# Reordering the first loads of a four-layer gated cross-attention kernel: eight small bias loads issued by ScalarE, the second and third context blocks ahead of most weights

## Chip, cores and metric

The kernel runs as one program on one core of a Trainium2 chip. The metric is the device time of one launch in microseconds (us), as the median of several runs. The core has five engines that run their own instruction streams: PE (TensorE: matmuls, with weight loads shown as PEld), DVE (VectorE), ACT (ScalarE), POOL (GpSimd) and SP (SyncE, which here only issues DMAs; its instruction queue is written SPq).

## What is computed

Four layers, each a gated cross-attention followed by a gated feed-forward block, on `x` of 16 batches of 128 tokens by 256 features, all in float32. Only the first attention matters for this change:

```
xn = layernorm(x)                                # per token, over 256 features
Q = xn @ Wq + bq;  K = ctx @ Wk + bk;  V = ctx @ Wv + bv       # 16 heads of 16
A = softmax(Q K^T / 4)
x = x + tanh(g_xattn[0]) * ((A V) @ Wo + bo)
```

After it follow a routed expert block (top 1 of 8), a second attention with a mask and an added bias, a routed block with top 2 of 8 and a shared expert, a third attention, a soft mixture over 64 experts, a fourth attention with heads of 64, and a product-key block.

## The kernel before

All 16 batches of `x` stay in SBUF as tiles `x0` to `x15` of 128 x 256. The context comes transposed, in four blocks of 512 columns (`ctxT`, block g holds batches 4g to 4g+3). The attention weights of a layer stand in one DRAM array `aw`, and are loaded into one large tile `aw` piece by piece.

**The loads.** `load_attention(0, load_others)` (L131) issues the first layer's loads, all on SP's queue, in the order in which they are written: the key weights (L135, 512 KB), context block 0 (L126, 512 KB), `x0` and `x1` (L58, 128 KB each), the two rows of gates (L63, L64), eight loads of query and key biases (L148, 16 partitions with 4 separate elements of 4 bytes each), the query weights (L151, 512 KB), the value weights (L152, 256 KB), the value bias and the output bias, each broadcast to all partitions (L153, L155), and then `load_others` (L178): `x2`, `x3`, context block 1, `x4`, `x5`, block 2, `x6`, `x7`, block 3, `x8`, `x9`. Eight loads of the output weights (L159) and `x10` to `x15` come last.

A load that the queue issues marks its end on one of eight completion slots, which are handed out in turn. A load whose slot was used before waits, in its issuing queue, until the load that had the slot has landed. All that stand behind it in the queue wait too.

**The work at the start.** POOL packs the key weights and later the query weights (L165). For each context block, `keys` (L436) multiplies packed key weights by the block into two PSUM banks `pk` (L442, four matmul instructions, each seen as two in the trace because the data are float32), and ACT adds the key bias into `kraw` (L445). POOL splits the keys into two masked halves `kT` (L454). For each batch: DVE takes mean and variance (L199, L201), POOL makes the reciprocal root (L194, L195), DVE writes the normalised tile `xn` (L226), POOL adds the gated output bias into `x` (L521), PE transposes `xn` (L237, `pt`), and ACT copies that out (L241). Then come queries (L461, L471), value rows (L487, L494), scores (L532), row maxima (L544), exponentials on ACT (L566), normalisation on POOL (L579), transposes (L585), values (L601), output (L617) and the gated sum (L259).

**The order.** In `xattn16` (L411) the order on each engine is written out by hand: a list of stages, each with a lag in batches, run under a manual schedule. Keys are in it ahead of everything: the order on PE is keys of block 0, keys of block 1, transpose of batch 0, keys of block 2, transpose of batch 1, keys of block 3, queries of batches 0 and 1, transpose of batch 2, value rows of batch 0, scores of batch 0. DVE scales the query bias (L171) and multiplies the output bias by the gate (L172) ahead of the first `xn`. POOL packs the query weights ahead of the first `kT` and the first reciprocal root. Engines run their instructions strictly in this order.

Of the kernel before, what the change touches and what calls it, by code (L numbers as in the profile page):

```python
# [22 lines left out]
NG, GT = 4, 512  # L23
# [13 lines left out]
def flamingo_gated(ctx: ExitStack, tc: tile.TileContext, a, out):  # L37
    nc = tc.nc
# [12 lines left out]
    def broadcast(ap, n):  # L51
        return ap.rearrange("(o n) -> o n", o=1).to_broadcast([P, n])
# [4 lines left out]
    def load_x(b):  # L57
        nc.sync.dma_start(out=xb[b], in_=a["x"][b])  # L58
# [3 lines left out]
    def load_gates():  # L62
        nc.sync.dma_start(out=gates[:, 0:4], in_=broadcast(a["g_xattn"], 4))  # L63
        nc.sync.dma_start(out=gates[:, 4:8], in_=broadcast(a["g_ffn"], 4))  # L64
        nc.scalar.activation(gates, gates, AF.Tanh)

    def gate_x(layer):
        return gates[:, layer : layer + 1]
# [55 lines left out]
    def load_context(g):  # L124
        t = ctxp.tile([P, 2, GT], F32, tag="ctxT", name="ctxT")
        nc.sync.dma_start(out=t, in_=a["ctxT"][:, :, g * GT : (g + 1) * GT])  # L126
        ctxT[g] = t
# [3 lines left out]
    def load_attention(layer, between=None):  # L131

        t = wp.tile([P, WSLOT], F32, tag="w", name=f"aw{layer}")
        src = a[f"aw{layer}"]
        nc.sync.dma_start(out=t[:, 1024:2048], in_=src[:, 1024:2048])  # L135
        if between is not None:
            load_context(0)
            for b in range(2):
                load_x(b)
            load_gates()  # L140
        bqk = t[:, 3328:3332].rearrange("p (n c) -> p n c", n=2)
        wo = t[:, 2560:3072].rearrange("p (c m) -> p c m", c=2)
        blocks = []
        for i in range(2):
            for j in range(4):
                blocks.append((i, slice(64 * i + 16 * j, 64 * i + 16 * (j + 1)), src[32 * j : 32 * j + 16, :]))
        for i, r, part in blocks:
            nc.sync.dma_start(  # L148
                out=bqk[r], in_=part[:, 3584:3592].rearrange("p (n c i) -> p n c i", n=2, c=2)[:, :, :, i]
            )  # L150
        nc.sync.dma_start(out=t[:, 0:1024], in_=src[:, 0:1024])  # L151
        nc.sync.dma_start(out=t[:, 2048:2560], in_=src[:, 2048:2560])  # L152
        nc.sync.dma_start(out=t[:, 3340:3596], in_=broadcast(a[f"bv{layer}"], D))  # L153
        tgbo = t[:, 3072:3328]
        nc.sync.dma_start(out=tgbo, in_=broadcast(a[f"bo{layer}"], D))  # L155
        if between is not None:
            between()
        for i, r, part in blocks:
            nc.sync.dma_start(  # L159
                out=wo[r], in_=part[:, 2560:3584].rearrange("p (c i m) -> p c i m", c=2, i=2)[:, :, i, :]  # L160
            )
        packed = {}
        for n, at in ((1, 3600), (0, 1024)):
            w = t[:, at : at + 512]
            nc.gpsimd.tensor_copy(  # L165
                w.rearrange("p (g d) -> p g d", d=16),
                t[:, n * 1024 : (n + 1) * 1024].rearrange("p (g s) -> p g s", s=32)[:, :, 0:16],
            )
            packed[n] = w.rearrange("p (c m) -> p c m", c=2)
        bq = t[:, 3332:3334]  # L170
        nc.vector.tensor_scalar(bq, bqk[:, 0, :], 0.25, None, ALU.mult)  # L171
        nc.vector.tensor_scalar(tgbo, tgbo, gate_x(layer), None, ALU.mult)  # L172
        aw[layer] = dict(
            wq=packed[0], wk=packed[1], wv=t[:, 2048:2560].rearrange("p (c m) -> p c m", c=2), wo=wo,
            bq=bq, bk=bqk[:, 1, :], bv=t[:, 3340:3596], tgbo=tgbo,
        )

    def load_others():  # L178
        for b in range(2, 10):
            load_x(b)  # L180
            if b % 2:
                if b // 2 < NG:
                    load_context(b // 2)

    load_attention(0, load_others)
    for b in range(10, B):
        load_x(b)
# [1408 lines left out]
    def attention1(after, joining):  # L1596
        load_attention(1)
        with tc.tile_pool(name="rel", bufs=3) as rp:
            loaded = {}

            def load(b):
                m = rp.tile([P, S], a["mask"].dtype, tag="m", name="m")
                nc.sync.dma_start(out=m, in_=a["mask"][b])
                r = rp.tile([P, S], F32, tag="r", name="r")
                nc.sync.dma_start(out=r, in_=a["rel"][b])
                loaded[b] = m, r

            def mask(b):
                mf = rp.tile([P, S], F32, tag="mf", name="mf")
                nc.gpsimd.tensor_scalar(mf, loaded[b][0], -1.0, HUGE, ALU.add, ALU.mult)  # L1610
                return mf

            def make(b, mf):
                r = loaded.pop(b)[1]
                f = rp.tile([P, 1], F32, tag="f", name="f")
                nc.vector.tensor_reduce(f, mf, AX.X, ALU.max)
                nc.vector.tensor_scalar(f, f, -1.0, None, ALU.is_ge)
                nc.vector.scalar_tensor_tensor(r, r, 0.25, mf, ALU.mult, ALU.add)
                return r, f

            xattn16(1, (load, mask, make), after, joining)
# [18 lines left out]
    def attention2(after, joining):  # L1640
        load_attention(2)
        xattn16(2, after=after, joining=joining)
# [99 lines left out]
```

## Time and profile before

| | us |
|---|---|
| median of three runs | 2056.13 (2055.76 to 2060.23) |
| the profiled execution | 2059.8 |
| its span, first to last instruction | 2058.1 |
| PE busy in the span | 1854.9 (90%) |
| DVE, ACT, POOL busy | 1257.9, 912.3, 791.2 |

The profile is of one execution. Times in it count from the start of the span. A timeline line reads: start, length, engine, line of the program, operation, result and operands, shapes, number of instructions merged; in square brackets the idle time of the engine ahead of it, and what ended that. A line of the waits view reads: engine and line that waited, what ended the wait, then us in total, times, and the longest. In a table by stretches, "PEclk" is the granted share of full TensorE clock and the last two columns are the mean busy share of the 16 DMA engines and the GB/s that they moved.

### The profile page before, as it was taken

What the parts mean: (1) busy time and instruction counts of PE and PEld (TensorE: products, weight loads), DVE (VectorE), ACT (ScalarE), POOL (GpSimd) and SP (SyncE); (2) the same over time, 40 slices, a digit from 0 to 9 for tenths busy, and PEclk for the clock granted to TensorE, in tenths of its full rate; (3) what the DMA queues carried; (4) which work ended last, traced back from release to release, by engine and by line L of the source; (5) the groups of instructions that cost most, each with busy time, mean ns of one, the idle gap of its engine ahead of it and who ended that gap; (6) DMA issues with size and microseconds to landing.
All of it is one profiled execution on the core that took longest, in us unless ns stands there. A gap on an engine that the chain in (4) does not pass through costs nothing.

```text
span 2058.1 us, 31016 instructions
## 1 busy us (share of the span) xinstructions
PE 1854.9 (90%) x10345; PEld 1242.7 (60%) x10345; DVE 1257.9 (61%) x3763; ACT 912.3 (44%) x3002; POOL 791.2 (38%) x952
## 2 busy tenths in 40 slices
PE   6996899979879999989979989868999999998787
PEld 3774566557636566657744434357776677775775
DVE  3885122478752222249859999699717666663797
ACT  4993222489911222249931122244324434333673
POOL 4873332377510455448832222200102222220785
PEclk9997999998889999999999999989999999999799
DMA  3003777310010688861031123433200000000000
GB/s 118 14 17 111 283 292 283 113 31 27 17 75 1 252 321 315 308 230 37 2 115 79 75 109 143 181 144 120 82 1 1 1 1 1 22 1 1 6 17 21
DMA packets 52720, 204.19 MB, mean 99 GB/s; under 512 B 11600, under 2 KB 31568, under 8 KB 41552
## 3 DMA queue, kind: packets, MB, share of 16 engines
q0 software_dynamic: 13872, 121.12, 16.1%
q1 hardware_dynamic: 38688, 81.07, 11.2%
q8 instruction: 84, 1.38, 0.3%
q14 instruction: 76, 0.62, 0.1%
HBM read 171.75 MB, written 30.41 MB: 98 GB/s over the span
## 4 chain that ended last, share of the span: by engine, by line
PE 27%; DVE 20%; issue 3%; ACT 3%; POOL 2%; DMA 1%; SPq 0%; POOLq 0%; ACTq 0%; DVEq 0%
PE pk L287 3%; PE pq L299 3%; PE po L382 3%; PE pv L310 3%; DVE tot L1317 2%; DVE rep L1523 2%; PE acc L1280 2%; PE po L1337 2%; PE av L372 2%; DVE cw L1311 1%; PE sc L329 1%; PE pq L1419 1%; DVE cw L1319 1%; PE pe L358 1%; PE pl L1254 1%
## 5 line engine op out<-in xcount | busy, mean ns | idle before, releaser
L922 PE MATMUL pg<-we,xT 128*128 128x512 f32 (+1 forms) x528 | 243.1, 590 | 2.4 <-ACT xT L211 2.4
L579 POOL TENSOR_TENSOR e<-e,sums 128x512 f32<-128x512 f32 x192 | 199.6, 1071 | 67.4 <-DVE sums L574 28.4
L928 DVE TENSOR_TENSOR h<-sg,pg 128x256 f32<-128x256 f32 x132 | 54.3, 411 | 237.7 <-ACT sg L927 190.1
L566 ACT ACTIVATE e<-sc,mx 128x128 f32<-128x128 f32 x512 | 181.5, 421 | 17.3 <-DVE mx L544 16.3
L927 ACT ACTIVATE sg<-pg 128x256 f32<-128x256 f32 x132 | 49.7, 376 | 270.3 <-PE pg L922 260.3
L888 POOL DMA_INDIRECT we<-in_we,rows x56 | 54.0, 964 | 265.6 <-PE pd L953 165.2
L350 POOL TENSOR_TENSOR e<-e,rec 128x512 f32<-128x512 f32 x64 | 65.3, 1041 | 219.0 <-DVE rec L349 155.2
L922 PEld LDWEIGHTS pg<-we,xT 128*128 128x128 f32 x528 | 96.2, 194 | 82.2 <-issue 72.1
L1337 PE MATMUL po<-yt,cT 128*128 128x256 f32 x512 | 126.1, 391 | 11.2 <-ACT cT L1329 11.1
L1280 PE MATMUL acc<-d,k 128*128 128x512 f32 x256 | 123.1, 623 | 13.9 <-POOL d L1270 13.5
L566 ACT ACTIVATION_READ_ACCUMULATOR e<-sc,mx 128x1 f32 x512 | 132.9, 260 | 0.0
L585 PE MATMUL pe<-ident,e 128*128 128x128 f32 x768 | 103.7, 279 | 32.0 <-DVE mx L549 17.4
L1270 POOL TENSOR_TENSOR d<-d,tot 128x1024 f32<-128x1024 f32 x32 | 62.8, 1961 | 174.0 <-DVE tot L1269 174.0
L953 PE MATMUL pd<-we,hT 128*128 128x256 f32 x528 | 127.2, 383 | 1.2 <-ACT hT L942 1.2
L1265 ACT ACTIVATE d<-d 128x1024 f32<-128x1024 f32 x32 | 33.8, 1057 | 200.8 <-DVE d L1264 178.9
L953 PEld LDWEIGHTS pd<-we,hT 128*128 128x128 f32 x528 | 98.4, 190 | 40.0 <-issue 23.7
L585 PEld LDWEIGHTS pe<-ident,e 128*128 128x128 f32 x768 | 86.0, 142 | 49.9 <-POOL e L579 24.6
L1254 PE MATMUL pl<-phi,xnT 128*128 128x512 f32 x256 | 116.1, 598 | 0.0
L1337 PEld LDWEIGHTS po<-yt,cT 128*128 128x128 f32 x512 | 95.6, 197 | 23.8 <-ACT cT L1329 12.6
L566 ACT ACTIVATE e<-e,mx 128x128 f32<-128x128 f32 x256 | 99.0, 397 | 0.3 <-DVE mx L549 0.3
L259 DVE SCALAR_TENSOR_TENSOR x<-po,gates,x 128x256 f32<-128x256 f32 x96 | 42.6, 444 | 92.5 <-PE po L382 54.2
L1280 PEld LDWEIGHTS acc<-d,k 128*128 128x128 f32 x256 | 48.9, 199 | 78.7 <-issue 53.3
(304 smaller groups left out, 4361.5 us busy)
## 6 DMA issues: line engine op xcount, KB each, us to landing
ew<-in_ew SPq DMA_DIRECT2D x8, 2048.0 KB
spill<-lg SPq DMA_DIRECT2D x32, 512.0 KB
cw<-spill SPq DMA_DIRECT2D x8, 2048.0 KB
got<-results SPq DMA_DIRECT2D x48, 128.0 KB
normed<-xn SPq DMA_DIRECT2D x32, 128.0 KB
aw<-in_aw SPq DMA_DIRECT2D x6, 512.0 KB
ctxT<-in_ctxT SPq DMA_DIRECT2D x4, 512.0 KB
x<-in_x SPq DMA_DIRECT2D x16, 128.0 KB
```

The lines of the kernel that those rows point to most:

```text
L287: nc.tensor.matmul(pk, lhsT=wk[:, k, c * P : (c + 1) * P], rhs=ctxT[g][:, k, :], start=(k == 0), stop=(k == 1))
L299: nc.tensor.matmul(pq[:, i * gt : (i + 1) * gt], lhsT=wq[:, k, (c + i) * P : (c + i + 1) * P], rhs=xnTs[g][:, k, :], start=(k == 0), stop= ...
L350: nc.gpsimd.tensor_tensor(e, e, rec.unsqueeze(2).to_broadcast([P, 4, S]), ALU.mult)
L566: nc.scalar.activation(e[:, c, :], sc[:, c, :], AF.Exp, bias=mx[:, h : h + 1], scale=sign, accum_out=sums[b][:, h : h + 1],)
L579: nc.gpsimd.tensor_tensor(e, e, r, ALU.mult)
L585: nc.tensor.transpose(pe[:, c * P : (c + 1) * P], e[:, c, :], ident)
L922: nc.tensor.matmul(pg[:, 0 : 2 * m].rearrange("p (g i) -> p g i", g=2), lhsT=tokens[j][:, k, :], rhs=wgu[:, k, :, i0 : i0 + m], start=(k = ...
L953: nc.tensor.matmul(pd[:, 0:D], lhsT=hT[0:m, ic, :], rhs=wd[0:m, ic, :], start=(ic == 0), stop=(ic == nic - 1))
L1254: nc.tensor.matmul(pl, lhsT=xnT[b // 4][:, k, tok], rhs=phi[:, k, n], start=(k == 0), stop=(k == 1))
L1270: nc.gpsimd.tensor_tensor(dv, dv, tot.unsqueeze(2).to_broadcast([P, 32, 32]), ALU.mult)
L1280: nc.tensor.matmul(acc[hf][k][q], lhsT=keep[b][:, k * P : (k + 1) * P], rhs=d[:, q * 512 : (q + 1) * 512], start=(b == 0), stop=(b == B - 1),)
L1337: nc.tensor.matmul(pos[b][:, 0:D], lhsT=cT[:, c, :], rhs=yt[2 * q + c // 2][:, c % 2, :], start=(q == 0 and c == 0), stop=(q == 3 and c == 3),
```

## The change

Only the order of the first layer's loads and the queue of eight of them change; layers 1 and 2 call the same function without `between` and load as before. The eight bias loads go to ScalarE's queue, ahead of everything else there. Block 0, `x0` and `x1` follow the key weights on SP as before, then come block 1, the gates, the query weights, `x2`, `x3`, block 2, and only then the value weights, the two broadcast biases, `x4`, `x5`, block 3, `x6` to `x9`, and the rest as before. Line numbers behind this place are 4 or 5 higher in the changed kernel.

```diff
         nc.sync.dma_start(out=t[:, 1024:2048], in_=src[:, 1024:2048])
-        if between is not None:
-            load_context(0)
-            for b in range(2):
-                load_x(b)
-            load_gates()
...
         for i, r, part in blocks:
-            nc.sync.dma_start(
+            (nc.sync if between is None else nc.scalar).dma_start(
                 out=bqk[r], in_=part[:, 3584:3592].rearrange("p (n c i) -> p n c i", n=2, c=2)[:, :, :, i]
             )
+        if between is not None:
+            load_context(0)
+            for b in range(2):
+                load_x(b)
+            load_context(1)
+            load_gates()
         nc.sync.dma_start(out=t[:, 0:1024], in_=src[:, 0:1024])
+        if between is not None:
+            for b in range(2, 4):
+                load_x(b)
+            load_context(2)
         nc.sync.dma_start(out=t[:, 2048:2560], in_=src[:, 2048:2560])
...
     def load_others():
-        for b in range(2, 10):
+        for b in range(4, 10):
             load_x(b)
-            if b % 2:
-                if b // 2 < NG:
-                    load_context(b // 2)
+            if b == 5:
+                load_context(3)
```

The completion slots are handed out anew with the order. In the changed kernel as it is built, `x0` waits for the slot of the key weights, `x1`, block 1, the query weights, `x2` and block 2 each for the slot of one of the bias loads, the first row of gates for that of block 0, and the output bias for that of the first row of gates. DVE's scaling of the query bias now stands ahead of the first variance; the orders on PE and POOL, and that of ACT behind its eight new loads, are the same as before.

## Prediction

> **What bounds it now.** The first line of the page is the frame: PE is busy for 90% of the span, so what a change of the first loads can give is time in which PE stands still or runs slowly at the start.
>
> ```profile
> PE 1854.9 (90%) x10345; PEld 1242.7 (60%) x10345; DVE 1257.9 (61%) x3763; ACT 912.3 (44%) x3002; POOL 791.2 (38%) x952
> ```
>
> Next the timeline of PE alone, 0 to 36 us.
>
> ```profile
> 7.41 6.18 PE L442 MATMUL pk<-ctxT,aw 128*128 128x512 f32 x8 [7.41 <-DMA ctxT<-in_ctxT]
> 17.60 6.22 PE L442 MATMUL pk<-ctxT,aw 128*128 128x512 f32 x8 [4.01 <-DMA ctxT<-in_ctxT]
> 23.66 0.38 PE L237 MATMUL pt<-ident,xn 128*128 128x128 f32 x2
> 23.87 3.60 PE L442 MATMUL pk<-ctxT,aw 128*128 128x512 f32 x8
> 27.31 0.38 PE L237 MATMUL pt<-ident,xn 128*128 128x128 f32 x2
> 27.53 3.60 PE L442 MATMUL pk<-ctxT,aw 128*128 128x512 f32 x8
> ```
>
> Keys of block 0 end at 13.6; PE waits 4.01 us for context block 1; keys of block 1 then take 6.22 us, where blocks 2 and 3, the same eight matmuls, take 3.60. From 17.60 to the first scores at 33.87 PE is never idle, so every later thing hangs on when block 1 is done. Stretches of 1 us show why that burst is slow: the granted clock falls to 0.50 about 2.3 us after PE went idle, and is full again only at about 22.65, 5.05 us after PE restarted.
>
> ```profile
> 14.00:15.00 1.00, 0.00 (x0) 0.00 (x0) 0.00 (x0) 0.31 (x1) 0.94 (x2) 1.00 1.03 353
> ...
> 16.00:17.00 1.00, 0.00 (x0) 0.00 (x0) 0.70 (x2) 0.00 (x0) 0.47 (x2) 0.50 1.06 374
> ...
> 22.00:23.00 1.00, 1.00 (x3) 0.53 (x2) 0.77 (x3) 0.10 (x1) 0.47 (x2) 0.65 0.59 177
> 23.00:24.00 1.00, 1.00 (x5) 0.48 (x4) 0.15 (x1) 0.14 (x1) 0.92 (x2) 1.00 0.22 57
> ```
>
> Why block 1 is late is in the timeline of SP:
>
> ```profile
> 3.55 0.43 SPq L64 DMA_DIRECT2D gates<-in_g_ffn  x1
> 4.02 5.46 SPq L148 DMA_DIRECT2D aw<-in_aw  x8
> 9.53 0.43 SPq L151 DMA_DIRECT2D aw<-in_aw  x1
> ...
> 11.43 0.90 SPq L58 DMA_DIRECT2D x<-in_x  x2
> 12.37 0.57 SPq L126 DMA_DIRECT2D ctxT<-in_ctxT  x1
> ```
>
> The bias loads hold SP from 4.02 to 9.48 (about 0.42 us each, the rest waits for completion slots, 1.9 of it for block 0), while the DMA engines stand at a share of 0.06 to 0.07 (7 to 10 us). Then weights go ahead of block 1, issued at 12.37.
>
> **The change, part by part.**
>
> *Eight bias loads to ACT.* SP loses 5.46 us. ACT gains 8 x 0.42 = 3.4 us of issue from about 0.8, with short slot waits: done by about 5. ACT's next work waits for the gates anyway (8.40 before), its first `kraw` for PE at 10.5, so this is hidden by 5 us of slack. No row shows a load issued by ACT, nor biases landing beside full-rate traffic. Before, the last bias (issued by 9.48) had landed at 11.03, so at most 1.55 us when quiet; gates, issued at 3.55 behind 1.3 MB, took till 8.40, 4.85 us. I take the quiet figure, nearer because on a queue of their own they have no megabyte ahead: the last lands by about 7. By the other end, 10 to 11: still free, since `kraw` waited till 11.20 before.
>
> *The start of PE.* It needs packed key weights (4.94) and block 0 (7.3). Gain bound: without `x0` and `x1` behind it block 0 might land as soon as its bytes have flowed, 1 MB at 290 GB/s from 1.75, near 5.4, and a tail: 0.9 us earlier. Loss bound: two SP issues each delayed by one ACT issue (0.43) and 8 bias loads' share of the DMA engines (0.07 x 5.5 us), together 1.3 us. I take 0.
>
> [...]
>
> *Block 1 early.* `x0` now waits for the slot of the key weights (landed 4.3), so SP issues: `x0` 4.3, `x1` 4.8, block 1 5.4 to 5.9, first gates 7.3 (slot of block 0), second 7.8, query weights 8.2, `x2`, `x3`, block 2 by 10.1, value weights 10.5, value bias 11.0, output bias 11.5, block 3 near 13.6 (0.43 to 0.55 each, as now). Bytes flow about 1 us after issue (9.53 to 10.5 for the query weights): block 1's from 6.4 at about 300 GB/s, drained at 8.2, landed by 9.7 with the 1 to 1.9 us that block 0 and the output bias took behind their bytes. PE needs it at 13.4: 3.7 us of slack. So the 4.01 us gap goes, PE never goes idle, and the clock, full since 12.4 in the first burst (the spacing of its weight loads falls from 0.85 to 0.43 us there), stays full: burst two takes 3.60 instead of 6.22, which is 2.6 us. It ends near 17.0 instead of 23.6. **Sum on PE: 4.0 + 2.6 = 6.6 us.**
>
> *What is late next.* The first transpose needs `xn` of batch 0. POOL's chain starts from `kraw` of block 0, which PE still ends at 13.6: `kraw` 14.3, `kT` 0.75, root 0.9, so `xn` at 16.0 to 16.4 (16.30 to 16.71 before). DVE must first multiply the output bias (15.45 before). Its load goes out 0.55 later than before (11.5 against 10.95), behind query weights, `x2`, `x3`, block 2 and value weights, 1.57 MB from 9.2 at 300 to 350 GB/s and then 0.26 MB more: landed between 15.0 and 16.6. So `xn` lies between 16.4 and 17.4, and PE loses 0 to 0.5. I take 0.4. This order was free before because PE came only at 23.66. `xn` 1 and 2 follow 2.95 us apart, for transposes at 20.9 and 26.5: covered by 1.5 us and more. Query weights (landed about 12.4) are packed ahead of the 14.3 that POOL waits for anyway. Block 2 lands near 15.5 against 17.3, block 3 near 18.9 against 21: covered.
>
> *Behind that.* From the first scores on, 27.6 instead of 33.87, no wait in the list for 34 to 180 us names a DMA, and ACT is 94% busy (16.9 to 18.7 of each 20 us), so the stage moves as a whole. The expert weights that follow are fetched by POOL only after routing (185 us); they move along.
>
> **Sum:** 6.6 - 0.4 = 6.2 us. Against the profiled execution, 2059.8 (1.7 of it outside the span of 2058.1), that makes 2053.6; the median of the runs is 3.7 lower, 2056.1, and gives **2049.9**. A measurement of this kernel can tell about 0.2%, 4.1 us, from no change.
>
> **Rivals.**
>
> 1. *The start slips.* ACT's issues and tiny packets delay key weights and block 0 (bound 1.3), and the output bias lands late (bound 1.5 more than taken). Gain 3.4 to 4.9: 2051 to 2053. For it: two queues have never run at once in this trace. Against: those 8 loads moved at a DMA share of 0.07.
>
> 2. *The clock opens later.* If the throttle's opening is not tied to PE's start, burst two may run partly cold. [...]
>
> 3. *Absorbed.* A later wait gives the time back: 2055 to 2057. It needs a deadline that does not move with the start; the waits behind 34 us show none.
>
> 4. *Slower.* The biases, on a queue beside full-rate traffic, land very late. All `kraw` wait for the last of them, POOL for `kraw`, and the first transpose comes 3.6 us after that landing. One us costs one us; the point where nothing is gained is a landing at 20 (11.03 before), and at 26 the time is 2062. Slot waits would add to it: block 1, query weights and block 2 wait for biases. Against: 1.55 us when quiet and 4.85 behind 1.3 MB are far from that.
>
> **How the numbers follow.** Forecast (gain of 5 to 7.5) 0.66; the start slips 0.12 (a quarter of it beyond 4.1); clock 0.06 (nearly all beyond); absorbed 0.08; slower 0.08. Faster 0.66 + 0.03 + 0.05 = 0.74, same 0.09 + 0.01 + 0.08 = 0.18, slower 0.08. The range: below, PE starting 0.9 earlier and no wait for `xn`, 7.5, to 2048.6, and 1.6 for the spread of runs: 2047. Above it takes in the late start, the clock and a part of the absorbed case: 2055.5. Left out are the slower case and a part of the absorbed one.
>
> **What would show it.** Right: on PE one burst of sixteen key matmuls from about 7.4 to 17, the granted clock at 1.00 from 13 on, the first scores at 27 to 28 and the first transpose near 17.2; SP's issue of block 1 before 6.5; no wait of PE on a context block but the first. Wrong: first matmul behind 8.5; `kraw` waiting for biases; block 1's issue held behind a bias; output bias landing behind 17.5; the end of the first attention (last value matmuls, near 172) moved by less than the first scores.

## The result

| | before | after |
|---|---|---|
| median (22 runs each) | 2056.09 us | 2054.01 us (2050.4 to 2057.06) |
| ratio after/before, 95% interval | | 0.9985 (0.9980 to 0.9991) |
| the profiled execution (span) | 2059.8 (2058.1) | 2055.99 (2054.3) |
| first scores on PE | 33.87 | 30.75 |

The change makes the kernel faster by 0.15%, some 3 us, about half of the forecast 6.2. The interval excludes no change at all, but the gain stays below the 0.2% that the prediction set as its bound, so by its own cases this is "same", to which it gave 0.18. The two medians differ by 2.1 us; the ratio of the comparison corresponds to 3.1.

First the engines' line of the changed kernel's page. PE is busy 3.0 us less than before. Only 0.45 of that lies ahead of the first scores (22.00 us busy up to there, 22.45 before); the rest lies behind them, in work that the change does not touch.

```profile
PE 1851.9 (90%) x10345; PEld 1240.6 (60%) x10345; DVE 1258.2 (61%) x3763; ACT 912.2 (44%) x3002; POOL 791.0 (39%) x952
```

The PE timeline of the changed kernel, as read before:

```profile
6.29 10.04 PE L446 MATMUL pk<-ctxT,aw 128*128 128x512 f32 x16 [6.29 <-DMA ctxT<-in_ctxT]
18.79 0.51 PE L241 MATMUL pt<-ident,xn 128*128 128x128 f32 x2 [2.46 <-DVE xn L230]
19.09 5.27 PE L446 MATMUL pk<-ctxT,aw 128*128 128x512 f32 x8
24.20 0.38 PE L241 MATMUL pt<-ident,xn 128*128 128x128 f32 x2
24.41 3.60 PE L446 MATMUL pk<-ctxT,aw 128*128 128x512 f32 x8
...
30.75 1.15 PE L536 MATMUL sc<-kT,qT 32*128 32x256 f32 x16
```

The two bursts have become one of sixteen matmuls; the gap of 4.01 is gone. But PE now stands idle for 2.46 us ahead of the first transpose, which before had no wait at all, and the keys of block 2 take 5.27 instead of 3.60. The table by stretches tells why: the granted clock closes (falls to half) at about 19.0, just when PE has restarted. Ahead of its first opening (the rise to full) the clock column prints 1.00, although PE runs slowly there: its weight loads come 0.85 us apart up to 11.54, and 0.43 from 12.30 on.

```profile
6.00:7.00 1.00, 0.71 (x1) 0.50 (x2) 0.00 (x0) 0.00 (x0) 0.00 (x0) 1.00 0.08 20
...
10.50:11.00 0.50, 0.50 (x2) 0.31 (x1) 0.00 (x0) 0.00 (x0) 0.00 (x0) 1.00 0.14 34
...
17.00:18.00 1.00, 0.00 (x0) 0.00 (x0) 0.00 (x0) 0.05 (x1) 0.28 (x1) 1.00 0.97 291
18.00:19.00 1.00, 0.21 (x2) 0.21 (x3) 0.94 (x3) 0.00 (x0) 0.19 (x1) 1.00 0.96 299
19.00:20.00 1.00, 1.00 (x4) 0.48 (x3) 0.25 (x2) 0.37 (x1) 0.92 (x2) 0.51 0.98 339
20.00:22.00 2.00, 2.00 (x4) 0.96 (x3) 0.72 (x2) 0.00 (x0) 1.31 (x4) 0.50 0.41 127
```

The account of the first scores, each term from the two PE timelines:

| term | us |
|---|---|
| PE starts earlier (6.29, was 7.41) | -1.12 |
| no gap ahead of block 1's keys | -4.01 |
| keys of blocks 0 and 1: 10.04, were 6.18 + 6.06 (to the first transpose) | -2.20 |
| wait ahead of the first transpose | +2.46 |
| clock closed in block 2's keys (24.20 - 18.79, was 27.31 - 23.66) | +1.76 |
| sum (the first scores themselves: -3.12) | -3.11 |

What the transpose waits for is the end of a chain. SP's timeline:

```profile
4.44 1.79 SPq L58 DMA_DIRECT2D x<-in_x  x2
6.34 0.57 SPq L126 DMA_DIRECT2D ctxT<-in_ctxT  x1
6.96 0.60 SPq L63 DMA_DIRECT2D gates<-in_g_xattn  x1
7.60 0.43 SPq L64 DMA_DIRECT2D gates<-in_g_ffn  x1
8.07 0.43 SPq L152 DMA_DIRECT2D aw<-in_aw  x1
...
11.45 0.71 SPq L160 DMA_DIRECT2D aw<-in_bo  x1
```

Then ACT, POOL and DVE, a fence each:

```profile
12.90 1.28 ACT L65 ACT_TABLE_LOAD   x1 [12.90 <-DMA x<-in_x]
14.20 0.21 ACT L65 ACTIVATE gates<-gates 128x8 f32<-128x8 f32 x1
14.31 1.83 ACT L449 ACTIVATE kraw<-pk,aw 128x512 f32<-128x512 f32 x3
```

```profile
14.65 0.61 POOL L170 COPY aw<-aw 128x512 f32<-128x512 f32 x1 [9.01 <-DMA aw<-in_aw]
15.67 0.70 POOL L458 TENSOR_SCALAR kT<-kraw,parity 128x512 f32<-128x512 f32 x1 [0.41 <-ACT kraw L449]
...
16.70 0.58 POOL L199 TENSOR_TENSOR rs<-ve,nhalf 128x1 f32<-128x1 f32 x1
```

```profile
18.06 0.35 DVE L177 TENSOR_SCALAR aw<-aw,gates 128x256 f32<-128x256 f32 x1 [9.59 <-DMA aw<-in_bo]
18.33 0.41 DVE L230 TENSOR_SCALAR xn<-x,mv,rs 128x256 f32<-128x256 f32 x1
```

Two holds stand one behind the other. The gates, issued at 6.96 and 7.60, release ACT's table load and tanh only at 12.90 (the view names a load of `x`, which a tanh of the gates does not need; in r1, the same kernel once more, it names the second row of gates, at 12.77). So the first `kraw` starts at 14.31, although PE had ended the keys of block 0 at about 12.7 (16.33 less the 3.6 of a burst at full clock), and POOL's root is done at 17.28. By then `xn` could run, but ahead of it on DVE stands the product of the output bias, and that load lands only at 18.06. `xn` and the transpose follow.

### The profile page after: what moved, and what is told of

It reads as the page before. It is cut to its first block, busy times and chain, and to the rows that moved or that the text cites. A ratio compares the mean times of both kernels' runs of the same rounds, so it can differ in the third digit from the quotient of the medians.

```text
span 2054.3 us, 31015 instructions
## 1 busy us (share of the span) xinstructions
PE 1851.9 (90%) x10345; PEld 1240.6 (60%) x10345; DVE 1258.2 (61%) x3763; ACT 912.2 (44%) x3002; POOL 791.0 (39%) x952
## 4 chain that ended last, share of the span: by engine, by line
PE 27%; DVE 20%; issue 4%; ACT 3%; POOL 2%; DMA 1%; POOLq 0%; ACTq 0%; DVEq 0%; SPq 0%
PE pk L291 3%; PE pq L303 3%; PE po L386 3%; PE pv L314 3%; DVE tot L1321 2%; DVE rep L1527 2%; PE po L1341 2%; PE acc L1284 2%; PE av L376 2%; DVE cw L1315 2%; PE sc L333 1%; PE pq L1423 1%; PE pl L1258 1%; DVE cw L1323 1%; DVE tot L1272 1%
```

## The experiments

Each edit is against the changed kernel. Theory A: the late output bias, with DVE's order, and the clock that closes in that wait take the missing half. Theory B: the gates, moved behind block 1, do it (late on SP's queue, late for ACT, and in the way of what follows). A third question is what the moved biases are worth by themselves. All ratios are to the kernel before, with the 95% interval. The medians belong to separate comparisons, in which the kernel before took 2056.09 (changed kernel), 2055.29 (e1 to e4), 2057.18 (e5 to e8) and 2056.85 us (e9, r1, r2), so compare the ratios. Only e5's interval is clear of the changed kernel's, by 0.0001; what the other runs show, they show in their traces, of one execution each.

| | first transpose (PE idle before it) | keys of block 2 | first scores | median us | ratio |
|---|---|---|---|---|---|
| changed kernel | 18.79 (2.46) | 5.27 | 30.75 | 2054.01 | 0.9985 (0.9980 to 0.9991) |
| e1 | 18.25 (1.70) | 3.60 | 28.52 | 2051.39 | 0.9980 (0.9972 to 0.9989) |
| e2 | 18.36 (3.23) | 3.60 | 28.64 | 2051.5 | 0.9983 (0.9974 to 0.9992) |
| e3 | 22.10 (none; 3.24 for block 1) | 3.60 | 32.31 | 2054.21 | 0.9995 (0.9987 to 1.0004) |
| e4 | 17.09 (0.32) | 3.70 | 29.88 | 2051.22 | 0.9979 (0.9971 to 0.9988) |
| e5 | 17.30 (0.72) | 3.60 | 27.57 | 2050.43 | 0.9966 (0.9953 to 0.9979) |
| e6 | 18.42 (1.79) | 3.60 | 28.69 | 2052.5 | 0.9978 (0.9969 to 0.9987) |
| e7 | 17.55 (2.35) | 3.60 | 27.82 | 2050.92 | 0.9973 (0.9964 to 0.9982) |
| e8 | 19.14 (3.25) | 6.33 | 32.34 | 2058.65, one run | |
| e9 | 16.69 (none) | 3.70 | 28.44 | 2051.61 | 0.9973 (0.9962 to 0.9983) |
| r1, changed kernel | 18.79 (2.92) | 4.79 | 30.45 | 2055.06, one run | |
| r2, as e2 | 18.51 (1.99) | 5.30 | 30.48 | 2055.87, one run | |

**e1: the output bias right behind block 1, ahead of the gates.**

```diff
             load_context(1)
+            nc.sync.dma_start(out=tgbo, in_=broadcast(a[f"bo{layer}"], D))
             load_gates()
...
-        nc.sync.dma_start(out=tgbo, in_=broadcast(a[f"bo{layer}"], D))
+        if between is None:
+            nc.sync.dma_start(out=tgbo, in_=broadcast(a[f"bo{layer}"], D))
```

> The changed kernel, with the load of the output bias moved ahead of the gates, right behind context block 1; nothing else. Theory A: the 2.46 us in which PE stands still ahead of the first transpose (18.79) and the slow clock behind it come from the output bias landing at 18.06. Then the first normalised tile waits only for POOL's root (17.28 in the changed kernel, some 0.4 later here as the gates go out behind 128 KB more): first transpose at 17.8 to 18.2, the clock stays full or nearly so, first scores at 28.3 to 29.2 instead of 30.75, time 1.5 to 2.5 us below the changed kernel, about 5 below before. Rival (the root is what holds it, since ACT's bias additions wait for the gates): first transpose at 18.2 or later, idle time of PE over 1.9, clock closes again, first scores 30 to 30.8.

The timeline of DVE in e1:

```profile
17.79 0.41 DVE L232 TENSOR_SCALAR xn<-x,mv,rs 128x256 f32<-128x256 f32 x1 [2.15 <-POOL rs L201]
```

The product now runs at 14.92 and is out of the way; `xn` waits for POOL's root instead. The transpose gains only 0.54, but the clock stays open, which is worth another 1.67, and the first scores gain 2.23. They are where theory A put them; the transpose, at 18.25, is just outside theory A's range and where the rival put it. What stands right behind the output bias is the root (done at 17.75), which waits for the gates (table load at 13.38) and for POOL's packing of the query weights (14.88).

**e2: the two gate loads on ScalarE's queue, behind its eight biases.**

```diff
-        nc.sync.dma_start(out=gates[:, 0:4], in_=broadcast(a["g_xattn"], 4))
-        nc.sync.dma_start(out=gates[:, 4:8], in_=broadcast(a["g_ffn"], 4))
+        nc.scalar.dma_start(out=gates[:, 0:4], in_=broadcast(a["g_xattn"], 4))
+        nc.scalar.dma_start(out=gates[:, 4:8], in_=broadcast(a["g_ffn"], 4))
...
         if between is not None:
+            load_gates()
             load_context(0)
...
-            load_gates()
```

> The changed kernel, with the two small gate loads issued by ScalarE behind the eight biases instead of by SP behind block 1. Theory B: on SP's queue these two loads (128 pieces of 16 bytes each) hold up all loads behind them, seen as a DMA share of 0.08 to 0.37 from 10.0 to 11.5 us, so that query weights, block 2 and the output bias land 1.5 to 2 us later than bytes need. Then here that hole is gone, gates have landed by 9, the first bias addition on ACT starts at once after PE (9.5 instead of 14.3), the output bias lands at 16 to 16.6, PE idles under 1 us ahead of the first transpose, the clock stays at 1.00, first scores at 27.0 to 28.0, time 6 to 7 us below before. Rival (bytes, not the gates, hold the queue): output bias at 17.5 or later, first scores 29.5 to 30.8. Rival (two queues contend): first matmul later than 6.8 instead of 6.29.

The timeline of ACT in e2:

```profile
6.76 0.69 ACTq L64 DMA_DIRECT2D gates<-in_g_ffn  x1
13.46 1.28 ACT L65 ACT_TABLE_LOAD   x1 [13.46 <-DMA gates<-in_g_ffn]
```

Missed. On a queue with nothing large ahead of them the gates land at 13.46 (12.91 in r2), no sooner than from SP's queue. So it is not their place in SP's queue that makes them late. The output bias lands at 17.08, 1.0 sooner than in the changed kernel, but only 0.28 sooner in r2 (17.78). The first scores came to 28.64 because in this execution the clock did not close, in spite of 3.23 us of idle; r2 shows that this is no property of the kernel.

**e3: the order of before, and only the eight biases on ScalarE's queue.** The edit is the changed kernel's one line `(nc.sync if between is None else nc.scalar)`, put into the kernel before.

> The kernel before, with only the eight bias loads moved to ScalarE's queue; the order on SP is otherwise that of before. If SP's time at the biases is most of the loss (5.46 us), block 1 lands about 4 us earlier and the first scores come near 29 to 30. My reckoning: block 1 still stands behind 1.3 MB (query and value weights, two biases, two tiles of x), lands near 15.5 to 16, PE idles over 2.3 us and the clock closes: keys of block 1 take 6.2, first scores at 31.5 to 32.5 instead of 33.87, 1.5 to 2.5 us below before.

As expected: PE starts at 6.15 but waits 3.24 us for block 1, and the clock closes as before (6.63 for its keys). 1.56 us on the first scores; in the time, nothing that the interval can tell from none.

**e4: the order of after, and the eight biases on SP, behind the gates.**

```diff
-        for i, r, part in blocks:
-            (nc.sync if between is None else nc.scalar).dma_start(
...
             load_context(1)
             load_gates()
+        for i, r, part in blocks:
+            nc.sync.dma_start(
```

> The changed kernel's order on SP, but with the eight bias loads on SP, behind the gates and ahead of the query weights. Keys of blocks 0 and 1 run as one burst, as in the changed kernel. But the biases wait for completion slots of block 1 and the gates, so the query weights go out near 12 and the output bias near 14.5; it lands near 20. Theory A: the first transpose comes at 20.5 to 21.5, the clock has closed, first scores at 32.5 to 35, time within 2 us of before. Rival (block 1 early is the whole gain): first scores 31 or earlier, 3 us below before.

Missed: 32.5 or later was expected. The timeline of PE in e4:

```profile
17.09 0.44 PE L241 MATMUL pt<-ident,xn 128*128 128x128 f32 x2 [0.32 <-DVE xn L230]
18.32 3.70 PE L446 MATMUL pk<-ctxT,aw 128*128 128x512 f32 x8 [0.79 <-DMA ctxT<-in_ctxT]
23.27 0.44 PE L241 MATMUL pt<-ident,xn 128*128 128x128 f32 x2 [1.25 <-DVE xn L230]
```

With block 1 early and the biases on SP the gain is there, even though the last bias lands only at 11.9. Three short waits (0.32, 0.79, 1.25) do less harm than one of 2.46, and none closes the clock. This run holds a second difference, however: DVE's product of the output bias came out behind the first `xn` (16.62; the product at 19.91). So it is to be held against e7, which has that order too and the biases on ScalarE. There PE waits neither for block 2 nor for the second `xn`, and the first scores come 2.06 sooner. Who issues the biases thus matters in the traces; the ratios (0.9979 and 0.9973) cannot tell the two apart.

**e5 and e6: the gates first on ScalarE's queue, the tanh behind the biases.** e5 also has e1's early output bias; e6 leaves that load where the changed kernel has it.

```diff
-        nc.sync.dma_start(out=gates[:, 0:4], in_=broadcast(a["g_xattn"], 4))
-        nc.sync.dma_start(out=gates[:, 4:8], in_=broadcast(a["g_ffn"], 4))
-        nc.scalar.activation(gates, gates, AF.Tanh)
+        nc.scalar.dma_start(out=gates[:, 0:4], in_=broadcast(a["g_xattn"], 4))
+        nc.scalar.dma_start(out=gates[:, 4:8], in_=broadcast(a["g_ffn"], 4))
...
+        if between is not None:
+            load_gates()
         for i, r, part in blocks:
...
         if between is not None:
+            nc.scalar.activation(gates, gates, AF.Tanh)
             load_context(0)
...
-            load_gates()
+            nc.sync.dma_start(out=tgbo, in_=broadcast(a[f"bo{layer}"], D))
```

> Both holds taken away: the two gate loads go out first on ScalarE's queue, ahead of the eight biases (tanh behind them), and the output bias goes out on SP right behind block 1. If the gates (through ACT's bias additions and POOL's root) and the output bias (through DVE) are all that stood between the keys of block 1 and the first transpose, gates land by 6, bias additions start with PE (9.7 and 12.8), POOL's root is done by 15 and the first transpose follows the sixteen key matmuls at 16.3 to 16.8 without idle time over 0.5; clock at 1.00 from then on; first scores 26.4 to 27.0, 6.9 to 7.5 below before (the forecast's 6.6 and the 1.1 by which PE starts earlier, less what is left). Rival: the query weights, which POOL packs ahead of the root, or the bytes of block 2 are next, first scores 27.5 or later.

The timeline of POOL in e5:

```profile
14.60 0.61 POOL L173 COPY aw<-aw 128x512 f32<-128x512 f32 x1 [8.04 <-DMA aw<-in_aw]
15.19 0.69 POOL L461 TENSOR_SCALAR kT<-kraw,parity 128x512 f32<-128x512 f32 x1
```

This is the best version, 0.9966. It falls short of the 26.4 to 27.0 expected (27.57), as its rival said: the table load is at 7.78 and the tanh at 9.07, so the gates are out of the way, but POOL waits for the query weights until 14.60, and `kT` and the root (done at 16.80) stand behind their packing.

> As the run before, but the output bias stays where the changed kernel has it. It tells the two holds apart: ACT and POOL are early (root by 15), and the first transpose waits for the output bias alone. It went out at 11.2 and landed at 17.1 with the gates on ScalarE behind the biases; here 16 to 17: first transpose at 16.8 to 17.8, clock stays full, first scores 27.0 to 28.0. If the gates were the whole cause of its late landing, 15 to 15.5 and no idle time.

The timeline of DVE in e6:

```profile
17.68 0.35 DVE L178 TENSOR_SCALAR aw<-aw,gates 128x256 f32<-128x256 f32 x1 [4.25 <-DMA aw<-in_bo]
```

With the gates early and the output bias as in the changed kernel, the root is ready at 16.55 and the output bias lands at 17.68; the transpose is at 18.42, only 0.37 sooner than in the changed kernel. 28.69 is 0.7 later than expected. So here the output bias holds the transpose alone, and the gates by themselves are worth little. The clock, this time, does not close after 1.79 us of idle.

**e7: the loads untouched; DVE's product of the output bias behind the first `xn`.**

```diff
-        nc.vector.tensor_scalar(tgbo, tgbo, gate_x(layer), None, ALU.mult)
+        if layer > 0:
+            nc.vector.tensor_scalar(tgbo, tgbo, gate_x(layer), None, ALU.mult)
...
             def output_bias(b):
+                if layer == 0 and b == 0:
+                    nc.vector.tensor_scalar(tgbo, tgbo, gate_x(layer), None, ALU.mult)
```

> The changed kernel's loads untouched; only DVE's multiplication of the output bias by its gate moves behind the first normalised tile. Theory A (that multiplication, waiting for the load, is what holds the first transpose): the output bias still lands near 18.06, but the first tile now follows POOL's root (17.28) at 17.3 to 17.4, first transpose at 17.8, PE idles 1.4 us, too short for the clock to close, first scores 28.0 to 28.6 instead of 30.75, time 2 to 2.7 below the changed kernel. If the load order by itself (bytes for block 2) is what costs, no change: 30.3 to 30.8.

The timeline of DVE in e7:

```profile
17.09 0.41 DVE L231 TENSOR_SCALAR xn<-x,mv,rs 128x256 f32<-128x256 f32 x1 [8.70 <-POOL rs L200]
17.64 0.35 DVE L527 TENSOR_SCALAR aw<-aw,gates 128x256 f32<-128x256 f32 x1
```

No load has moved, and the first scores come 2.93 us sooner (27.82, expected 28.0 to 28.6): 1.24 from the transpose, 1.67 from a clock that stays open. `xn` runs as soon as the root is there, and the product right behind it. The 1.24 is the cleanest proof of theory A: the one wait on DVE, not the bytes, was what the output bias cost (0.23 of it is a root that was done sooner here, at 17.05). The 1.67 is not the edit's alone: PE idles 2.35 us here and the clock stays open, while in r2 it closed with 1.99.

**e8: the load of the gates doubled.** Two more loads of the same rows, into a tile that nobody reads, directly behind the two on SP.

```diff
+    more = const.tile([P, 8], F32, name="more")
...
+        nc.sync.dma_start(out=more[:, 0:4], in_=broadcast(a["g_xattn"], 4))
+        nc.sync.dma_start(out=more[:, 4:8], in_=broadcast(a["g_ffn"], 4))
```

> The changed kernel with two more gate loads of the same form, into a tile that nothing reads, on SP right behind the two. It prices these small loads. If each holds the queue behind it beyond its 0.43 us of issue (a hole of 1.5 us in the DMA share for two), the output bias lands 1.5 to 2 us later, at 19.5 to 20, and the first scores come at 32 to 33. If only issue counts: 18.5 to 19, scores 31.2 to 31.7. If they are hidden: 18.1, 30.8.

The timeline of DVE in e8:

```profile
18.41 0.35 DVE L180 TENSOR_SCALAR aw<-aw,gates 128x256 f32<-128x256 f32 x1 [9.95 <-DMA aw<-in_bo]
```

Missed: the output bias is issued 1.44 later (12.89) but lands only 0.35 later. In e7, with the loads of the changed kernel, it had landed by 17.64, when the product starts, so executions with the same loads differ by as much. The cost of two more small loads is not clear of that spread, and theory B's "in the way of what follows" is small. Its other half, late for ACT, stands: the gates decide when `kraw` starts. The 32.34 is mostly the clock, closed during all of block 2's keys (6.33).

**e9: large loads first.** SP issues key weights, block 0, `x0`, block 1, query weights, then the eight biases, `x1`, the output bias, block 2 and the rest; the gates on ScalarE's queue; the product as in e7.

```diff
+            load_gates()
             load_context(0)
-            for b in range(2):
-                load_x(b)
+            load_x(0)
             load_context(1)
...
         nc.sync.dma_start(out=t[:, 0:1024], in_=src[:, 0:1024])
         if between is not None:
+            biases()
+            load_x(1)
+            nc.sync.dma_start(out=tgbo, in_=broadcast(a[f"bo{layer}"], D))
+            load_context(2)
             for b in range(2, 4):
                 load_x(b)
-            load_context(2)
```

> Built from what the runs before it showed: gates first on ScalarE's queue; on SP the large loads that the start needs, one behind the other on fresh completion slots (key weights, block 0, x0, block 1, query weights), then the eight biases on SP, then x1, the output bias, block 2; DVE's multiplication of the output bias behind the first normalised tile. Block 0 has traffic behind it again, so PE starts near 7.4; query weights land by 11 instead of 14.6, the last bias near 12, POOL's root near 15.7, so the first transpose follows the key matmuls at 16.3 to 17 without a wait over 0.4; clock full; first scores 26.6 to 27.3 (27.57 in the best kernel so far), 6.6 to 7.2 below before. Rival: block 2, behind the biases, lands later than 17.5 and PE waits for it: scores 28 or later.

28.44 instead of 26.6 to 27.3. The query weights are packed from 11.04, and the transpose at 16.69 waits for nothing; but the biases, which in this program wait for the slots of earlier loads (the last of them for that of the query weights), held SP from 3.85 to 11.24, the last bias landed at 12.58, PE started at 7.96, and block 3 came 1.00 late. Each order of these loads that was tried has a next one that is late.

**r1 and r2: the changed kernel and e2 once more.**

> The changed kernel once more, for its trace. If the late start of the transpose belongs to the kernel, the output bias lands at 17.5 to 18.6 again, and PE idles 2 to 3 us. [...]

> The kernel with the gates on ScalarE behind the biases once more, for its trace. There PE idled 3.23 us, longer than the 2.46 of the changed kernel, and yet the clock stayed full. Fixed idle time cannot give both. [...]

In r1 the output bias lands at 18.06 again and the clock closes again: the late transpose belongs to the kernel. In r2 PE was idle for less time than in e2 (1.99 against 3.23), and yet the clock closed, as its table by stretches shows:

```profile
18.00:19.00 1.00, 0.49 (x3) 0.49 (x4) 0.97 (x4) 0.01 (x1) 0.47 (x1) 0.92 1.02 350
19.00:20.00 1.00, 1.00 (x2) 0.42 (x2) 0.01 (x1) 0.36 (x1) 0.92 (x2) 0.50 1.02 344
```

Same program as e2, where block 2's keys took 3.60; here they take 5.30. The first transpose in the PE timelines, r2 and then e2:

```profile
18.51 0.44 PE L241 MATMUL pt<-ident,xn 128*128 128x128 f32 x2 [1.99 <-DVE xn L230]
```

```profile
18.36 0.44 PE L241 MATMUL pt<-ident,xn 128*128 128x128 f32 x2 [3.23 <-DVE xn L230]
```

What differs is where the idle time lies. In the traces of before and after each of the 53 stretches of one granted clock, the last of a trace excepted, lasts a whole number of 3.41 us (3.41 to 378.88), and where the tables by stretches of r1, r2 and e3 show a closing and the next opening, these lie 3.4, 3.4 and 6.8 us apart. So the changes of the clock measured here lie on a grid of 3.41 us, and where it lies differs from one execution to the next: the closings at 15.87 (before), 19.02 (after), 18.24 (r1) and 18.83 (r2) are 2.2, 2.0, 1.2 and 1.8 us more than a multiple of 3.41. Cut along the grid, r2 has its 1.99 us of idle inside one stretch (3.41 less the 1.42 of PE), and the clock closes at its end:

```profile
15.42:18.83 3.41, 1.42 (x6) 0.51 (x5) 1.02 (x4) 1.42 (x3) 1.76 (x4) 1.00 1.01 348
18.83:22.25 3.42, 3.42 (x7) 1.36 (x6) 1.11 (x4) 0.37 (x1) 2.61 (x5) 0.50 0.63 192
```

In e2 the grid, counted on from the opening at 9.8, has an edge at 16.65, which cuts the 3.23 us into 1.51 and 1.72, and the clock stays open:

```profile
13.23:16.65 3.42, 1.91 (x5) 0.57 (x3) 0.00 (x0) 3.18 (x6) 1.04 (x2) 1.00 1.04 361
16.65:20.06 3.41, 1.70 (x6) 0.98 (x7) 1.28 (x4) 0.99 (x3) 2.58 (x6) 1.00 0.94 324
```

Up to the first scores the other executions agree. In the six in which the clock closed, the stretch of 3.41 us that ended there held 1.99 us of idle or more (r2 1.99, before 2.28, e3 2.35, r1 2.37, e8 2.39, the changed kernel 2.46). It stayed open with 1.72 in e2 and with 1.70 and 1.79 in all in e1 and e6. In e7 it stayed open too, with 2.35 in all; where the edge lies there is an estimate (opening about 4.0 us behind the first matmul, from a burst of 9.10 against e2's 8.86 with 3.5): near 16.9, which leaves 1.75 in one stretch. (Later in the kernel, under other matmuls, the clock also closed with as little as 0.7, at 172.6 in the changed kernel, where PE is busy for 2.70 of the 3.41 us ahead of it.) So whether 2 to 3 us of idle cost another 1.7 us depends on where the grid lies. An edit does not set that: it is chance, and a part of the spread between runs.

## Why the prediction was right, and where it was wrong

- **The time, and luck.** 2054.0 lies in the range of 2047 to 2055.5, but the sum behind the forecast of 2049.9 does not hold: 6.2 us forecast, 3.12 at the first scores. Against its terms, the start of PE brought 1.12 more and the burst 0.4 less, the wait ahead of the transpose cost 2.06 more, and the clock behind it 1.76. That the time is still in the range is in part luck: the early start was not counted on, and the upper end was drawn for a late start, a clock that opens late in block 1's keys, and a gain that is absorbed. One sign that the prediction named for being wrong came, an output bias landing behind 17.5 (18.06). Of its signs for being right, the first scores at 27 to 28, the transpose near 17.2 and a clock that stays at 1.00 did not come.
- **Right: block 1 early, and the gap.** SP issued block 1 at 6.34 (forecast before 6.5), the gap of 4.01 went in full, and one burst of sixteen replaced two. e4 and e3 put the gain there: the order without ScalarE's queue gives 0.9979 (with DVE's product behind the first `xn`, however), the biases alone 0.9995.
- **Right: the clock in that burst.** Forecast 2.6, measured 2.2. Block 1's keys ran at full clock, as forecast, but the clock opened at 12.2, 5.9 us after the first matmul and not 5.05, which cost 0.4 in block 0's. This size is partly chance: in the ten executions with one burst of sixteen the clock opened 3.5 to 6.1 us after the first matmul.
- **Right: the biases on ACT are hidden.** Issued by 4.93; DVE scales the query bias at 7.38, so those had landed (forecast: about 7). The slower rival's late biases are not seen.
- **The start of PE was taken as unchanged and gained 1.12,** a little beyond the bound of 0.9. The reason given for that bound is what happened: `x0` waits until 4.44 for its slot (2.5 us, until the key weights had landed), and block 0 lands without `x0` and `x1` beside it. The kernels whose `x0` goes out late (4.4 to 5.4) start at 6.11 to 6.88; before, e4 and e9, with `x0` out at 1.97 or 1.98, at 7.41, 7.36 and 7.96. The prediction's loss by two queues at once did not come: SP's first two issues took 0.39 and 0.67 beside ACT's, 0.39 and 0.68 alone, so neither of the two delays of 0.43 in that bound shows.
- **Wrong: "What is late next".** This is the step that failed. It forecast the root at about 16.0, the output bias landed between 15.0 and 16.6, and took 0.4 for the wait of PE. Measured: root 17.28, output bias 18.06, wait 2.46. In e7, where the root alone held it, the transpose came 0.50 behind the end of the root; a root done at 17.28 would thus have given about 17.78. So about 1.45 of the 2.46 is the root (17.78 less 16.33) and 1.0 the output bias. The step named the right instruction and the right queue ahead of it. It failed in three sizes:
  - *The gates.* "ACT's next work waits for the gates anyway" was read from before, where they landed at 8.40, so that the tanh was done by 9.9 (8.40 + 1.28 + 0.21), ahead of the keys at 10.5. Moved, they landed at 12.90 (5.3 us behind the second issue), and ACT's table load, tanh and all `kraw` wait for them. The move was costed at nothing. With the gates first (e5) the table load is at 7.78. But this is the smaller part of the late root: with the gates first it was done at 16.80 (e5) and 16.55 (e6), only 0.5 to 0.7 sooner, because it then stood behind the query weights.
  - *Landing times.* The sum spread bytes at 300 to 350 GB/s over the queue. But the DMA engines stand at a share of 0.08 from 6 to 7 us and 0.14 to 0.25 from 10 to 11.5: the large loads are spaced out. So query weights landed at 14.65 instead of 12.4, and the output bias 1.5 behind the far end of its bounds.
  - *The clock, a second time.* The sum priced the idle time and not what it would do to the clock behind it: 1.76 more in this execution.
- **Rivals.** The first is half of what happened: the output bias made the transpose 1.6 later than forecast (18.79 against 17.2; it allowed 1.5), but the start did not slip. The second put the clock in the wrong burst: block 1's keys ran at full clock, and block 2's lost 1.76. No run shows what a late opening in block 1's keys would cost, which the upper end of the range and the chances take in; what the runs showed in its place is the closing ahead of block 2's keys. Its condition, an opening that is not tied to PE's start, holds (3.5 to 6.1 us). What the traces show is the grid of 3.41 us, and an outcome that hangs on where the idle time lies in it (e2 and r2). The prediction's 2.3 us to close and 5.05 to open count from where PE stopped and started; from one change of the clock to the next it is 6.83 us in the kernel before (15.87 to 22.70, read as 22.65 in the prediction), twice 3.41. The third, absorbed, is refuted: first scores 3.12 sooner, first value matmul 48.6 to 45.5, the routing's DMA 184.8 to 181.7, the last instruction on PE 2054.4 to 2050.6. The last value matmuls of the first attention moved by 3.06 (171.32 to 168.26). Over all timed kernels the shift of the first scores divided by 2056 gives the ratio to within 0.0008 (1.6 us): e5 -6.30 is 0.9969 (measured 0.9966), e3 -1.56 is 0.9992 (0.9995).
- **Open.** How the hole from 10 to 11.5 us divides between small loads on SP's queue and waits for completion slots is not settled: e8 says that two loads more cost no more than 0.35, and without the gates on SP the output bias landed 1.0 (e2) and 0.28 (r2) sooner. The mean DMA share in that hole is 0.19 to 0.25 in the changed kernel, r1, e7 and e8, but 0.90 in e2 and 0.52 in r2, so the gates on SP have a part in it. A larger number of slots was not tried.

## What to carry to other kernels

When a large load is moved ahead, list what is pushed behind it, small constants above all: one that gates a table load or a product in program order ahead of the critical tile can take back half of the gain (here 2 KB of gates and a broadcast bias). Issue such constants first, or move their use behind the work that doesn't need them; e7 brought the transpose 1.24 us forward without touching a load. And price an idle stretch of PE of 2 us or more with the clock's closing beside it, as a risk: in the six executions here in which it closed, the eight matmuls behind it took 1.2 to 3.0 us longer. An idle stretch of 1.79 us or less never closed it in this place.

## What the runs showed of the hardware

- Small loads landed late beside bulk traffic, whichever queue issued them: gates of 2 KB issued by SP at 6.96 and 7.60 landed by 12.90 (the changed kernel), issued by ACT at 6.35 and 6.76 at 13.46 (e2), 6.7 us behind the second issue with nothing large on that queue, against at most 1.55 for the last bias behind DMA engines at a share of 0.06 to 0.07 (before). As the first loads of all, issued at 0.80 and 1.23, they landed at 6.19 (e9).
- Completion slots: in the traces of before and after the loads at the start end on eight semaphores in turn, small ones too (in the kernel before the first load at 4.27, and the ninth on the same semaphore at 8.85), and SP's queue shows the waits for them. In the kernel before a bias load waited 1.9 us until block 0 had landed, and in the changed kernel `x0` was held from about 2 to 4.44 us, until the key weights had; block 0, with nothing behind it, landed 1.1 us sooner. In e9 eight bias loads of 0.2 KB held SP for 7.39 us.
- Granted clock: the first burst of sixteen key matmuls took 8.86 (e2) to 10.12 us (e1) in ten executions, against 7.2 at full clock (twice 3.60), so the opening varies between executions: 3.5 us (e2) to 6.1 us (e1) behind the first matmul, and 5.1 in r2, the same program as e2.
- Every change of the granted clock in the traces of before and after lies on a grid of 3.41 us. From its closing ahead of the first scores to its next opening it took 3.41 us in the changed kernel, 3.4 in r1 and r2, 6.83 in the kernel before, 6.8 in e3, and over 5.7 in e8 (closed at 18.28, not open by 24). In this place it closed with 1.99 us or more of PE's idle time inside one stretch of the grid, and 3.23 us that an edge cut in two (e2) did not close it.
